# ConvNeXt block and Mamba block on one core: the first conv pairs written ahead of the weights' setup, and the first batch's MLP with its eight halves interleaved

## The chip, the core and the metric

The kernel runs on one core of one Trainium2 chip. A core has five engines with their own instruction queues: TensorE (PE, matrix products; its weight loads are listed as PEld), VectorE (DVE), ScalarE (ACT), GpSimd (POOL) and SyncE (SP), which here issues nearly all DMA transfers. Each engine works through its queue in order and waits on semaphores for the others. The metric is the device time in microseconds (us), smaller is better. The time before is 17438.78 us, the median of three runs (17432.75 to 17440.56).

## The reference

Two layers run one after the other on x of shape 32 x 96 x 56 x 56. The first is a ConvNeXt block, the second a Mamba block with two scan layers, a pooled branch, a 1x1 fusion and a batch norm. The change touches only the first layer:

```python
h = conv7x7_depthwise(x, conv_w) + conv_b          # one filter per channel
h = transpose(h, (0, 2, 3, 1))                     # channels last
h = (h - mean(h)) * rsqrt(var(h) + 1e-5) * ln_g + ln_b     # over the 96 channels
h = gelu(h @ w1 + b1)                              # 96 -> 384
h = h @ w2 + b2                                    # 384 -> 96
x = transpose(h, (0, 3, 1, 2)) * layer_scale + x
```

The second layer takes this x, batch by batch, through layer norm, projection, a causal conv of four taps, and a scan along the 3136 positions. Its pooled branch needs the mean of x over all positions of a batch.

## The kernel before

**Program order.** The kernel is written with a framework that orders the instructions of each engine at build time. Outside the loop that order is the framework's: of the instructions whose inputs are there it takes the one written first, so an instruction that waits for nothing can move far ahead of its place in the text. The loop at the end (L962 on) is under a manual order, in which the text is the order.

**Setup (L114 to L243).** Loads and prepares all weights: identity matrix, selection matrices, the layer norms' gains folded into the projections (`norm_weights`), the second layer's weights twice. Nearly all tiles are in the pool `const` and live to the end. Scratch is in `su`, with two PSUM banks in `sups`. Every transfer is issued by SP.

**First conv (L257 to L326).** The batches are split into groups: batches 0 to 10 (b0 = 11) first, then three groups of 7. For the first group the depthwise conv runs in front of the loop. The channels go in 48 pairs. For a pair p, 112 partitions hold two channels x 56 rows. A band matrix T of 112 x 7 x 112 holds the 7 x 7 filter (one 112 x 112 block per column offset dw). It is built on DVE with seven `copy_predicated` instructions, under seven masks that POOL makes once (three `affine_select` each, L269 to L277). Then PE multiplies, for two parts of the batches, seven shifted images with the seven blocks (L318), and ACT adds the bias and evicts (L322). The transfers of a pair are: the image into xpad (L302), the band out to DRAM for the later groups (L312) and the result out (L326). Band and image have three buffers each, used in turn. The conv's weights (cw, L288, and the bias cb, L289) are loaded with each filter repeated over the 56 rows. The pools `cc` (SBUF), `cx` and `cp` (six PSUM banks) open after the setup's pools are closed.

**MLP of a batch (`block0`, L383).** Batch b, chunk c (of four), half s (of two): 392 positions each. It is cut into pieces: load (conv result), load_x (input), center (L355), square (L360), mean (L365), root (Ln and Exp, L371 and L372), norm (L419), up (three products, L424), gelu (three activations, L432), down (L439 and L443), residual (L450, and the store of a chunk, L455). For the last half of a batch come total, pool and fuse, which make the pooled branch's bias `fb`. Each piece has a slot number, which says where in the loop it is put. For the batches 1 to 31 these pieces run inside the loop, one half per stage. For batch 0 they are written in front of the loop (L939), half by half, each half's pieces in the order of their slots. The tiles come from the loop's pool `wp` (cv, xin and gl with one buffer each) and from the loop's PSUM tags ps0, ps1 and ps2, with one bank each.

**First preparation and loop.** `prep` (L541) of the first stage runs next: it loads seq (the stored result of the MLP), norms and projects it. Then the loop runs 256 stages of 24 steps: each step is an Exp on ACT, a product and a scan on DVE (L878, L885) and a product on POOL (L889), and PE sums up (L922). The last part (L996 on) computes the batch norm and writes the output.

Of the kernel before, what the change touches and what calls it, by code (L numbers as in the profile page):

```python
# [34 lines left out]
F32 = mybir.dt.float32  # L35
I32 = mybir.dt.int32
AF = mybir.ActivationFunctionType
ALU = mybir.AluOpType
AX = mybir.AxisListType
PSUM = bass.MemoryType.PSUM  # L40
DRAM = bass.MemoryType.DRAM

H = W = 56
L = H * W
C = 96
# [6 lines left out]
NCH = 4  # L52
CH = L // NCH
HC = CH // 2
ROWS = HC // W
FF = 384
NF = FF // 128
# [4 lines left out]
def convnext_mamba_kernel(  # L62
# [31 lines left out]
    nc = tc.nc  # L94
# [3 lines left out]
    const = ctx.enter_context(tc.tile_pool(name="const", bufs=1))  # L98
# [3 lines left out]
    b0 = B - 3 * NB if B > 3 * NB else B  # L102
    groups = [(0, b0)] + [(b, b + NB) for b in range(b0, B, NB)]
    conv_d = [
        dram.tile([C * H, (hi - lo) * W], F32, name=f"conv_d{lo}", tag=f"conv_d{lo}")
        for lo, hi in groups
    ]
    band_d = dram.tile([C // 2, 2 * H, 7 * 2 * H], F32, name="band_d")
    stats_d = dram.tile([C, B * NCH, 4], F32, name="stats_d")
    x1_d = [dram.tile([C, L], F32, name=f"x1_d{b}", tag=f"x1_d{b}") for b in range(B)]  # L110
    o_d = [dram.tile([C, L], F32, name=f"o_d{b}", tag=f"o_d{b}") for b in range(B)]


    setup = ExitStack()  # L114
# [80 lines left out]
    for i in range(2):  # L195
# [12 lines left out]
        if i == 1:  # L208

            d["res"] = fw1  # L210
            for q in range(NQ):
                ps = sups.tile([128, 512], F32, name="ps", tag="nps")
# [40 lines left out]
        nc.vector.memset(t[C : C + 1, :], 1.0)  # L253
        hn0s.append(t)


    R2 = 2 * H  # L257
    GB = (b0 + 1) // 2
    cb = const.tile([R2, C // 2], F32, name="cb")
    with tc.tile_pool(name="cc", bufs=1) as cc, tc.tile_pool(name="cx", bufs=3) as cx, tc.tile_pool(  # L260
        name="cp", bufs=6, space=PSUM
    ) as cps:
        ones = cc.tile([R2, R2], F32, name="ones")
        nc.vector.memset(ones, 1.0)
        masks = []
        for dh in range(7):
            m = cc.tile([R2, R2], F32, name="m", tag="m", bufs=2)

            nc.gpsimd.affine_select(  # L269
                out=m, in_=ones, compare_op=ALU.is_equal, fill=0.0, base=3 - dh,  # L270
                pattern=[[-1, R2]], channel_multiplier=1,
            )
            nc.gpsimd.affine_select(
                out=m[:, 0:H], in_=m[:, 0:H], compare_op=ALU.is_ge, fill=0.0, base=H - 1,
                pattern=[[0, H]], channel_multiplier=-1,
            )
            nc.gpsimd.affine_select(  # L277
                out=m[:, H:R2], in_=m[:, H:R2], compare_op=ALU.is_ge, fill=0.0, base=-H,
                pattern=[[0, H]], channel_multiplier=1,
            )  # L280
            mi = cc.tile([R2, R2], I32, name=f"mi{dh}", tag=f"mi{dh}")
            nc.vector.tensor_copy(mi, m)
            masks.append(mi)
        cw = cc.tile([R2, C // 2, 49], F32, name="cw")
        wv = conv_w.rearrange("(p two) k -> two p k", two=2)
        bv = conv_b.rearrange("(p two) k -> two p k", two=2)
        for j in range(2):
            nc.sync.dma_start(cw[j * H : (j + 1) * H], wv[j].partition_broadcast(H))  # L288
            nc.sync.dma_start(  # L289
                cb[j * H : (j + 1) * H].unsqueeze(2), bv[j].partition_broadcast(H)  # L290
            )
        bands, xpads = [], []
        for i in range(3):
            t = cc.tile([R2, 7, R2], F32, name=f"band{i}", tag=f"band{i}")
            nc.gpsimd.memset(t, 0.0)
            bands.append(t)
            t = cc.tile([R2, b0, W + 6], F32, name=f"xpad{i}", tag=f"xpad{i}")
            nc.gpsimd.memset(t, 0.0)
            xpads.append(t)
        for p in range(C // 2):  # L300
            xp, T = xpads[p % 3], bands[p % 3]
            nc.sync.dma_start(  # L302
                xp[:, :, 3 : 3 + W],
                x[0:b0, 2 * p : 2 * p + 2, :].rearrange("b c (h w) -> (c h) b w", w=W),
            )
            for dh in range(7):
                nc.vector.copy_predicated(
                    T,
                    masks[dh].unsqueeze(1).broadcast_to([R2, 7, R2]),
                    cw[:, p, dh * 7 : (dh + 1) * 7].unsqueeze(2).broadcast_to([R2, 7, R2]),  # L310
                )
            nc.sync.dma_start(band_d[p], T.rearrange("p k n -> p (k n)"))  # L312
            ct = cx.tile([R2, b0 * W], F32, name="ct")
            for lo in range(0, b0, GB):
                n = min(GB, b0 - lo)
                ps = cps.tile([R2, GB * W], F32, name="ps")
                for dw in range(7):
                    nc.tensor.matmul(  # L318
                        ps[:, 0 : n * W], T[:, dw, :], xp[:, lo : lo + n, dw : dw + W],
                        start=(dw == 0), stop=(dw == 6),  # L320
                    )
                nc.scalar.activation(  # L322
                    ct[:, lo * W : (lo + n) * W], ps[:, 0 : n * W], AF.Identity,
                    bias=cb[:, p : p + 1],
                )
            nc.sync.dma_start(conv_d[0][p * R2 : (p + 1) * R2, :], ct)  # L326


    with ExitStack() as main:
        wp = main.enter_context(tc.tile_pool(name="wp", bufs=2))  # L330
        pp = main.enter_context(tc.tile_pool(name="pp", bufs=3, space=PSUM))
        pu = main.enter_context(tc.tile_pool(name="pu", bufs=1, space=PSUM))
        py = main.enter_context(tc.tile_pool(name="py", bufs=1, space=PSUM))
        bcd = main.enter_context(tc.tile_pool(name="bcd", bufs=3, space=DRAM))

        def psum(k):

            return pp.tile([128, 512], F32, name="ps", tag=f"ps{k}", bufs=1)

        def halves(t):  # L340
            return t.rearrange("p (a b) -> p a b", a=2)
# [14 lines left out]
            return ps  # L356

        def squared(ps):
            sq = wp.tile([R2, HC], F32, name="sq", tag="sq", bufs=3)[0:C]
            nc.scalar.activation(sq, ps[0:C, 0:HC], AF.Square)  # L360
            return sq

# [17 lines left out]
        batch_sums = {}  # L380
        xins = {}

        def block0(b, c, s):  # L383
# [2 lines left out]

            def load():
                if k == 0:
                    batch_sums[b] = wp.tile([C, NCH * 2], F32, name="sums", tag="sums", bufs=2)
                v["cv"] = wp.tile([C, ROWS, W], F32, name="cv", tag="cv", bufs=1)  # L390
                g = 0 if b < b0 else 1 + (b - b0) // NB
                at = (b - groups[g][0]) * W
                nc.sync.dma_start(
                    v["cv"],
                    conv_d[g].rearrange("(c h) w -> c h w", h=H)[
                        :, k * ROWS : (k + 1) * ROWS, at : at + W
                    ],
                )

            def load_x():  # L400
                if s == 0:
                    xins[b, c] = wp.tile([C, CH], F32, name="xin", tag="xin", bufs=1)
                    nc.sync.dma_start(xins[b, c], x[b, :, c * CH : (c + 1) * CH])

            def center():
# [21 lines left out]
                    )  # L427

            def gelu():
                v["gl"] = wp.tile([128, NF, HC], F32, name="gl", tag="gl", bufs=1)  # L430
                for f in range(NF):
                    nc.scalar.activation(  # L432
                        v["gl"][:, f], v["pss"][f][:, 0:HC], AF.Gelu, bias=b1_sb[:, f : f + 1]
                    )
                exp_ln_tables()
# [20 lines left out]


            def total():
                v["m"] = wp.tile([C, 1], F32, name="mean", tag="gps")
                nc.vector.tensor_reduce(v["m"], batch_sums[b], AX.X, ALU.add)  # L460

            def pool():
                ps = psum(2)
                nc.tensor.matmul(ps[0:C, 0:1], gpw_sb, v["m"], start=True, stop=True)
                v["gp"] = wp.tile([C, 1], F32, name="gp", tag="gps")
                nc.scalar.activation(v["gp"], ps[0:C, 0:1], AF.Relu, bias=gpb, scale=1.0 / L)

            def fuse():
                ps = psum(2)
                nc.tensor.matmul(ps[0:C, 0:1], fw2, v["gp"], start=True, stop=True)  # L470
                fb = wp.tile([C, 1], F32, name="fb", tag="fb", bufs=3)
                nc.scalar.activation(fb, ps[0:C, 0:1], AF.Identity, bias=fusb)
                batch_bias[b] = fb

# [3 lines left out]
                (12.8, root), (14.1, True, norm), (15.6, up), (15.9, gelu), (17.3, down),  # L478
                (18.3, residual),
            ]  # L480


        xpad = wp.tile([R2, NB, W + 6], F32, name="xpad", tag="xpad", bufs=1)
# [452 lines left out]
            for _, piece in sorted(where.pop(n, ()), key=lambda p: p[0]):  # L936
                piece()

        for c in range(NCH):  # L939
            for s in range(2):  # L940
                for slot, *piece in sorted(block0(0, c, s), key=lambda p: p[0]):
                    piece[-1]()
        for slot, *piece in sorted(prep(stages[0]), key=lambda p: p[0]):
            if slot < 24:
                piece[-1]()
# [143 lines left out]
```

## Time and profile before

| What | us |
|---|---|
| median of three runs | 17438.78 |
| the profiled execution | 17446.45 |
| its span | 17444.6 |
| up to the last setup transfer's issue | 48.73 |
| DVE's first band copy | 93.19 |
| PE's first conv product | 105.43 |
| first load of the MLP of batch 0 | 463.42 |
| last residual of batch 0 | 595.87 |
| first norm of the first preparation | 600.41 |
| first scan of the loop | 643.23 |

Times in the table are from the start of the profiled span. Over the whole span DVE is busy 92%, POOL 89%, PE 89% and ACT 66% of the time, but these are averages over stages with different limits. The stages in front of the loop have to be looked at by themselves. In the lines that follow, a name such as `ps<-cv,center_m` means output from inputs, with the buffers' numbers left out; `x8` counts instructions; the bracket at the end gives how long the engine was idle before, and what released it. Some names occur twice, as digits are left out: `cb<-in_conv_b` is the conv's bias, `cb<-in_mconv_b` that of the second layer. SPq is SP's queue: a transfer's time there is that of its issue, not of its data.

### The profile page before, as it was taken

To read this page: it belongs to the slowest core of one execution; us is meant where nothing else is said; L and a number is where in the kernel's file an instruction comes from. 1 tells how busy PE (TensorE), PEld (TensorE's weight loads), DVE (VectorE), ACT (ScalarE), POOL (GpSimd) and SP (SyncE) were. 2 spreads that over 40 slices of the span, in tenths; PEclk is the share of its full clock that TensorE was granted. 3 is DMA by queue.
4 is the path that set the end of the run, shared out by engine and by line. 5 is a ranking of instruction groups with operands and counts; after the bars stand their busy time and mean duration, and the time that the engine had idled before them with its cause. 6 is when DMAs were issued, how large, how long until landed. Compare 5 with 4: busy or idle time off the path is not lost. (4 is left out here: it accounts for less than half of the span.)

```text
span 17444.6 us, 217495 instructions
## 1 busy us (share of the span) xinstructions
PE 15502.9 (89%) x67992; PEld 5472.5 (31%) x67992; DVE 16064.8 (92%) x12345; ACT 11460.0 (66%) x18647; POOL 15605.6 (89%) x8737
## 2 busy tenths in 40 slices
PE   7799999999999999999999988888888888888870
PEld 5233333333333333333333322222222222222220
DVE  7499999999999999999999999999999999999994
ACT  1566766666666666666666666666666666666653
POOL 0499999999999999999999999999999999999991
PEclk9799999999999999999999999999999999999985
DMA  4355555555555555555555555555555555555548
GB/s 101 87 141 138 141 138 136 138 140 139 140 135 139 138 139 139 136 137 138 139 140 138 134 126 130 127 125 126 126 129 128 125 126 126 129 127 124 127 115 276
DMA packets 1421981, 2346.44 MB, mean 135 GB/s; under 512 B 629958, under 2 KB 793586, under 8 KB 1420820
## 3 DMA queue, kind: packets, MB, share of 16 engines
q1 hardware_dynamic: 1413652, 2294.00, 53.7%
q10 hardware_dynamic: 7168, 38.54, 0.6%
q8 instruction: 536, 8.78, 0.2%
q14 instruction: 625, 5.12, 0.1%
HBM read 1929.11 MB, written 402.41 MB: 134 GB/s over the span
## 5 line engine op out<-in xcount | busy, mean ns | idle before, releaser
L889 POOL TENSOR_TENSOR da<-h,bc 128x784 f32<-128x784 f32 x6144 | 11267.2, 1856 | 855.6 <-DVE h L885 734.9
L885 DVE TENSOR_TENSOR_SCAN h<-da,st,w 128x784 f32<-128x784 f32 x3072 | 5664.5, 1844 | 326.4 <-ACT st L896 8.6
L922 PE MATMUL y<-da,ssum 128*32 128x392 f32 x24576 | 5147.1, 542 | 407.2 <-POOL da L889 403.2
L878 DVE TENSOR_TENSOR w<-w,bc 128x784 f32<-128x784 f32 x4096 | 3996.2, 976 | 300.9 <-PE w L851 132.7
L862 POOL TENSOR_TENSOR da<-us,bc 128x784 f32<-128x784 f32 x2048 | 3819.1, 1865 | 2.3 <-DMA us<-uu 2.3
L836 ACT ACTIVATE da<-d,A 128x784 f32<-128x784 f32 x4096 | 3757.4, 941 | 43.1 <-DMA d<-dd 27.3
L836 ACT ACTIVATE w<-d,A 128x784 f32<-128x784 f32 x2048 | 1878.3, 918 | 2635.0 <-DVE h L885 2285.8
L885 DVE TENSOR_TENSOR_SCAN h<-w,st,da 128x784 f32<-128x784 f32 x1536 | 2712.2, 1827 | 5.9 <-ACT w L836 4.8
L587 PE MATMUL ps<-hn,wx 97*64 97x392 f32 x12288 | 2265.9, 503 | 7.4 <-DVE hn L575 7.4
L922 PEld LDWEIGHTS y<-da,ssum 128*32 128x32 f32 x24576 | 1094.8, 115 | 3681.1 <-issue 2141.1
L885 DVE TENSOR_TENSOR_SCAN h<-da,w 128x784 f32<-128x784 f32 x1024 | 1827.0, 1784 | 109.1 <-ACT st L896 4.3
L851 PE MATMUL w<-u,sel 64*128 64x392 f32 x4096 | 1026.5, 580 | 655.0 <-DVE h L885 654.0
L587 PEld LDWEIGHTS ps<-hn,wx 97*64 97x64 f32 x12288 | 793.7, 137 | 1434.5 <-issue 1117.3
L666 POOL TENSOR_TENSOR u<-dl,xc 128x784 f32<-128x784 f32 (+1 forms) x512 | 737.5, 1440 | 564.1 <-ACT dl L652 564.1
L916 PE MATMUL y<-xc,D 128*128 128x392 f32 x1536 | 802.2, 608 | 257.1 <-DVE z L903 249.4
L506 PE MATMUL ps<-xpad,band 112*112 112x224 f32 (+1 forms) x4032 | 1003.0, 358 | 0.0
L351 ACT ACT_TABLE_LOAD x759 | 973.8, 1283 | 14.3 <-PEq L1076 0.8
L885 DVE TENSOR_TENSOR_SCAN h<-w,da 128x784 f32<-128x784 f32 x512 | 872.3, 1766 | 0.0
L360 ACT ACTIVATE sq<-ps 96x392 f32<-96x392 f32 x768 | 340.7, 490 | 797.3 <-PE ps L355 448.9
L506 PEld LDWEIGHTS ps<-xpad,band 112*112 112x112 f32 x4032 | 583.7, 175 | 832.5 <-issue 770.0
L644 PE MATMUL ps<-dbl,dtw 6*64 6x392 f32 x3072 | 685.7, 509 | 99.6 <-ACT dbl L622 99.6
L851 PEld LDWEIGHTS w<-u,sel 64*128 64x128 f32 x4096 | 327.9, 196 | 1255.6 <-DVE h L885 1096.3
(124 smaller groups left out, 14444.6 us busy)
## 6 DMA issues: line engine op xcount, KB each, us to landing
bc<-bd SPq DMA_DIRECT2D x4096, 196.0 KB, 5.3
d<-dd SPq DMA_DIRECT2D x6144, 98.0 KB, 2.9
us<-uu SPq DMA_DIRECT2D x2048, 98.0 KB, 2.2
dd<-dl SPq DMA_DIRECT2D x512, 294.0 KB, 3.8
uu<-u SPq DMA_DIRECT2D x1024, 49.0 KB, 1.6
band<-band_d SPq DMA_DIRECT2D x144, 343.0 KB, 3.6
cv<-conv_d SPq DMA_DIRECT2D x256, 147.0 KB, 2.5
xin<-in_x SPq DMA_DIRECT2D x128, 294.0 KB, 4.2
```

Of the source, the lines that this page charges most:

```text
L351: nc.scalar.preload_act_table_set("natural_log_exp_and_others")
L506: nc.tensor.matmul(v["ps"][0:R2, 0 : (last - first) * W], v["band"][:, dw, :], xpad[:, first:last, dw : dw + W], start=(dw == 0), stop=(dw ...
L587: nc.tensor.matmul(v["x", q][rows(a), 0:HC], weights[:, k, 64 * q : 64 * q + 64], v["hn"][:, o : o + HC], start=(k == 0), stop=(k == last),)
L666: nc.gpsimd.tensor_tensor(S.u[:, lo:hi], v["dl"][:, lo:hi], S.xc[:, lo:hi], ALU.mult)
L836: nc.scalar.activation(e, S.d4[j], AF.Exp, scale=S.d["A"][:, j, g : g + 1])
L851: nc.tensor.matmul(S.u4[:, 512 * a : 512 * a + HC], sel[rows(a), j % 2, :], S.u[rows(a), j // 2, :], start=True, stop=True,)
L862: nc.gpsimd.tensor_tensor(t, S.us[j], S.bcs[g][:, 0, :], ALU.mult)
L878: nc.vector.tensor_tensor(halves(db), S.u4.rearrange("p (a b) -> p a b", a=2)[:, :, 0:HC], halves(S.bcs[g][:, 0, :]), ALU.mult,)
L885: nc.vector.tensor_tensor_scan(ring[:, g, :], S.e.pop((j, g)), db, 0.0 if c == 0 else d["st"][:, j, g : g + 1], ALU.mult, ALU.add,)
L889: nc.gpsimd.tensor_tensor(da, ring[:, g, :], S.bcs[g][:, 1, :], ALU.mult)
L916: nc.tensor.matmul(S.y[:, 0:HC], S.d["D"][:, q, :], S.xc[:, q, :], start=True, stop=False)
L922: nc.tensor.matmul(S.y[r0 : r0 + 32, 0:HC], ssum, da[:, tok(a)], start=False, stop=(g == NG - 1),)
```

## The change

The block of the first conv, from its pools up to the images' memsets, moves ahead of the setup, and the body of its loop over pairs becomes a function `conv_pair(p)`. Three pairs are written before the setup, the other 45 after it. The pools stay open in between, beside those of the setup, in an `ExitStack`. The MLP of batch 0 gets an SBUF pool `p0` with three buffers for each of its tiles and a PSUM pool `pp0` with eight banks of one tag, which are closed before the loop's pools are opened. Its pieces are no longer written half after half. All are sorted by their slot plus 3 for each half.

```diff
+    first_conv = ExitStack()
+    cc = first_conv.enter_context(tc.tile_pool(name="cc", bufs=1))
+    cx = first_conv.enter_context(tc.tile_pool(name="cx", bufs=3))
+    cps = first_conv.enter_context(tc.tile_pool(name="cp", bufs=6, space=PSUM))
...
+    for j in range(2):
+        nc.sync.dma_start(cw[j * H : (j + 1) * H], wv[j].partition_broadcast(H))
+        nc.sync.dma_start(
+            cb[j * H : (j + 1) * H].unsqueeze(2), bv[j].partition_broadcast(H)
+        )
...
+    def conv_pair(p):
+        xp, T = xpads[p % 3], bands[p % 3]
...
+    for p in range(3):
+        conv_pair(p)
+
+
     setup = ExitStack()
     su = setup.enter_context(tc.tile_pool(name="su", bufs=2))
     sups = setup.enter_context(tc.tile_pool(name="sups", bufs=2, space=PSUM))
...
-        for p in range(C // 2):
-            xp, T = xpads[p % 3], bands[p % 3]
...
+    for p in range(3, C // 2):
+        conv_pair(p)
+    first_conv.close()
...
     with ExitStack() as main:
-        wp = main.enter_context(tc.tile_pool(name="wp", bufs=2))
-        pp = main.enter_context(tc.tile_pool(name="pp", bufs=3, space=PSUM))
-        pu = main.enter_context(tc.tile_pool(name="pu", bufs=1, space=PSUM))
-        py = main.enter_context(tc.tile_pool(name="py", bufs=1, space=PSUM))
-        bcd = main.enter_context(tc.tile_pool(name="bcd", bufs=3, space=DRAM))
-
+        pre = []
         def psum(k):
 
+            if pre:
+                return pre[1].tile([128, 512], F32, name="ps", tag="pre", bufs=8)
             return pp.tile([128, 512], F32, name="ps", tag=f"ps{k}", bufs=1)
+
+        def work(shape, name, bufs):
+
+            pool, n = (pre[0], 3) if pre else (wp, bufs)
+            return pool.tile(shape, F32, name=name, tag=name, bufs=n)
...
-                v["cv"] = wp.tile([C, ROWS, W], F32, name="cv", tag="cv", bufs=1)
+                v["cv"] = work([C, ROWS, W], "cv", 1)
...
-                v["gl"] = wp.tile([128, NF, HC], F32, name="gl", tag="gl", bufs=1)
+                v["gl"] = work([128, NF, HC], "gl", 1)
...
-                fb = wp.tile([C, 1], F32, name="fb", tag="fb", bufs=3)
+                fb = (
+                    const.tile([C, 1], F32, name="fb0")
+                    if pre
+                    else wp.tile([C, 1], F32, name="fb", tag="fb", bufs=3)
+                )
...
+        with tc.tile_pool(name="p0", bufs=1) as p0, tc.tile_pool(
+            name="pp0", bufs=1, space=PSUM
+        ) as pp0:
+            pre += [p0, pp0]
+            pieces = [
+                (slot + 3 * (2 * c + s), piece)
+                for c in range(NCH)
+                for s in range(2)
+                for slot, *_, piece in block0(0, c, s)
+            ]
+            for _, piece in sorted(pieces, key=lambda p: p[0]):
+                piece()
+            pre.clear()
+
+        wp = main.enter_context(tc.tile_pool(name="wp", bufs=2))
+        pp = main.enter_context(tc.tile_pool(name="pp", bufs=3, space=PSUM))
...
-        for c in range(NCH):
-            for s in range(2):
-                for slot, *piece in sorted(block0(0, c, s), key=lambda p: p[0]):
-                    piece[-1]()
         for slot, *piece in sorted(prep(stages[0]), key=lambda p: p[0]):
```

The lines left out move unchanged. xin, sums, sq, and the two small tiles of the pooled branch are switched to `work` in the same way as cv and gl.

## The prediction

> **What bounds the kernel now.** I read three views, from coarse to fine. First, the busy time of each engine in stretches that I cut at the kernel's own joints: setup, the convolution's weights, the first conv pairs, the conv, the MLP of batch 0, the first preparation, the loop. Columns: microseconds from the span's start, length, then busy time (and instruction count) of each engine, granted TensorE clock, DMA share, GB/s.
>
> ```profile
> core 0: us, PE busy (x) PEld busy (x) DVE busy (x) ACT busy (x) POOL busy (x), PEclk, DMA share, GB/s
> 0.00:48.73 48.73, 7.22 (x20) 2.97 (x20) 11.69 (x46) 2.36 (x6) 0.70 (x6) 1.00 0.20 38
> 48.73:93.19 44.46, 0.59 (x4) 0.30 (x4) 3.88 (x14) 0.85 (x4) 8.15 (x27) 1.00 0.30 34
> 93.19:105.43 12.24, 0.00 (x0) 0.03 (x1) 12.24 (x14) 0.00 (x0) 0.00 (x0) 1.00 0.28 36
> 105.43:463.42 357.99, 354.74 (x1344) 236.55 (x1344) 330.25 (x323) 49.71 (x96) 0.00 (x0) 1.00 0.45 119
> 463.42:596.36 132.94, 90.50 (x151) 35.69 (x152) 4.88 (x9) 60.69 (x88) 0.00 (x0) 0.63 0.12 30
> 596.36:640.00 43.64, 34.30 (x130) 13.05 (x129) 2.39 (x5) 24.21 (x36) 1.84 (x1) 0.73 0.39 100
> 640.00:17240.00 16600.00, 15015.56 (x66348) 5183.90 (x66345) 15632.83 (x11899) 11259.58 (x18383) 15594.92 (x8703) 0.94 0.55 134
> ```
>
> The loop is 16600 of 17444.6 us, held by DVE and POOL (both 94%), and the change does not write into it. What it touches is the first 640 us: 93 us in which no compute engine does much, 358 us of conv with PE full, and 133 us of MLP in which nothing is full (PE 68% at a granted clock of 0.63, ACT 46%). All of it precedes the loop's first scan (643.23), so what is saved there is saved at the end.
>
> Second, the timeline at the start of the conv (start, duration, engine, line, operation; in brackets the idle time before and its releaser):
>
> ```profile
> 48.73 13.00 SPq L289 DMA_DIRECT2D cb<-in_conv_b  x2
> ...
> 62.05 24.15 SPq L288 DMA_DIRECT2D cw<-in_conv_w  x2
> 86.24 6.71 SPq L302 DMA_DIRECT2D xpad<-in_x  x3
> 93.19 7.39 DVE L307 COPY_PREDICATED band<-mi,cw 112x784 f32<-112x784 int32 x8 [33.99 <-DMA cw<-in_conv_w]
> ...
> 116.10 0.33 SPq L302 DMA_DIRECT2D xpad<-in_x  x1
> ```
>
> SP's queue is the limit here: setup's transfers are issued from 0.80 to 48.7 without a break (48 us), then 44 us for bias, conv weights and the first three images. DVE waits 34 us for cw.
>
> Third, one half of the MLP:
>
> ```profile
> 483.58 1.28 ACT L371 ACT_TABLE_LOAD   x1
> ...
> 484.87 0.55 ACT L371 ACTIVATE ps<-ps,eps_c 96x392 f32<-96x392 f32 x1
> 485.44 1.28 ACT L372 ACT_TABLE_LOAD   x1
> 486.74 0.47 ACT L372 ACTIVATE ps<-ps 96x392 f32<-96x392 f32 x1
> 487.23 1.28 ACT L432 ACT_TABLE_LOAD   x1
> 487.25 0.56 DVE L419 TENSOR_TENSOR hz<-cv,ps 96x392 f32<-96x392 f32 x1 [15.59 <-ACT ps L372]
> 487.86 0.50 PEld L424 LDWEIGHTS ps<-hz,w_sb 97*128 97x128 f32 x2 [4.00 <-DVE hz L419]
> 487.86 4.29 PE L424 MATMUL ps<-hz,w_sb 97*128 97x392 f32 x6 [3.35 <-DVE hz L419]
> ...
> 498.01 0.58 ACT L450 ACTIVATE xin<-ps,b2ls 96x392 f32<-96x392 f32 x1 [5.24 <-PE ps L443]
> ```
>
> It is one chain: each engine waits for the one before, and the next half's center waits for this residual, since both use the PSUM tile of tag ps2. A half lasts 18.5 us the first time and 16.4 on average after (463.42 to 596.36: 132.9 = 18.5 + 7 x 16.4).
>
> **The conv's weights first.** Issue of cw, cb, cw, cb costs 24.15 + 13.00 = 37.2 us wherever it stands; moved to the head it runs from 0.8 to 38. The second cw is through after 0.8 + 12.1 + 6.5 + 12.1 = 31.5 and lands 7 us later, as now (86.2 to 93.19): copies from about 38.5 instead of 93.2, the three image loads from 38 to 44.7, PE 12.2 us after the copies (as now, 93.19 to 105.43) at 50.7. The three pairs take 22 us (a pair is 7.33: ACT's rows of L322 repeat every 7.32), to 73. POOL's 27 mask and memset instructions (8.15 us) move under the wait for cw; the ident that setup needs stands behind them, but setup's transfers are issued only 40 us later, so this is free.
>
> But setup's 48 us of issue did not go away. It is written ahead of pairs 3 to 47, and its transfers wait for nothing, so I take them to stand on SP before the image of pair 3: 44.7 + 48 + six stores of pairs 0 to 2 (0.3 to 0.4 each, 2 us) = 95, plus 4.3 us to land (the median of that load) = 99. Pair 3 starts now at 105.43 + 22 = 127.4. Gain 28. DVE executes in order, and setup's last operations wait for the last setup transfers; if copies for pair 3 stand behind them they start at 97 and pair 3 at 104 or later. Setup's other DVE work (46 instructions, 11.7 us, till now under DMA waits) fits into the idle time from 73 to 97; without that cover it costs its 11.7 us, since in the conv DVE is 92% busy. PE's and ACT's setup work (7 and 2 us) lies in the same gap. **I take 25**. Ends: 0, if setup's transfers or its DVE work stand ahead of pair 0 (SP then ends where it ends now); 42, if the images of pairs 3 and on slip between setup's transfers (105.4 - 50.7 less 12 for DVE).
>
> The pools cost nothing: conv and setup now hold 6 + 2 PSUM banks together, and conv's memsets no longer wait for setup's tiles.
>
> **The MLP interleaved.** Tiles get 3 buffers and 8 PSUM tiles, and pieces are sorted 3 slots apart, so two to three halves are under way at once. The chain no longer decides, the fullest engine does. ACT per half: 0.49 (square) + 0.55 + 0.47 + 3 x 0.59 (gelu) + 0.58 + 0.19 (residual) = 4.05, and three table loads of 1.28 = 3.85: 7.9, which the window of each half confirms. PE: 18 passes of 0.33 us at full clock (the second center to down of 576.98 on) = 5.9, of 0.65 at half clock = 11.8.
>
> Two rules bear on this. The row first: a table load takes 1.28 us and the Ln after it starts 10 ns later. The Trainium skill, "ScalarE: Activation LUTs", section on what ACT_TABLE_LOAD costs, gives 1283 ns plus a drain of about 1380, and advises to do all work of one set before switching; interleaving does the opposite. With 2.66 us per switch a half would be 4.05 + 8.0 = 12 and the saving at the stage's end 31; with the row's 1.28 it is 59. The row decides, as no such drain shows in it. The advice keeps its point, though: gelus of one half come 0.65 us apart on PE, and the next half's Ln or Exp can fall between them; each such break is one more 1.28. At most five loads per half (Ln, Exp and three gelus all apart) give 10.5. I count one extra: **9.2 us per half**.
>
> The clock: now PE idles 3.35 us before each up, and up's passes run at 0.65. "TensorE: Matmul & The Clock Gate", Part 1, says the clock halves after an idle window of some 3.4 us and comes back after a busy one; with no such gap left PE would need 5.9 per half and ACT alone would bind. The row nearest in density, 596 to 640 (PE 79% busy), was granted only 0.73, where 18 passes last 0.33 / 0.73 x 18 = 8.1. Both are under 9.2, so I keep 9.2; only at half clock throughout would PE set 11.8.
>
> Sum: first half 18.5, then 7 x 9.2 = 64.4, together 83 instead of 133: 50 saved. Ends: 7.9 per half, 59; 11.8, 32.
>
> **What is given back.** Now the first preparation (seq loads, center, square, mean) runs inside the last half: center<-seq at 589.8, and its first norm at 600.41, 4 us after the residual. In the change the loop's pools open after the MLP's close, so seq's load waits for fuse: total, pool and fuse 2 us, load 2.5, center to Exp 5.5 (1.3 + 0.5 + 1.3 + 0.55 + 1.28 + 0.47): norm at 10 us after the residual. **Minus 6** (2 to 10). The fb0 tile and the hoisted preloads (L351, one load at 0.80) cost nothing.
>
> **Sum:** 25 + 50 - 6 = 69. The profiled execution took 17446.45 us (span 17444.6, 1.85 around it), 7.7 over the median of the runs, 17438.78; its 69 come off the median: **17370**.
>
> **Rivals.** *Forecast* as above, 0.60, its own range 17350 to 17390. *Conv runs through*: SP leaves room for the later images; 42 + 50 - 6 = 86, 17353. For it: SP needs only 1.15 us per pair; against: order of writing. 0.16. *PE stays slow and setup goes first*: PE at half clock, 32, minus 6, plus 5: 31, 17408. For it: a clock of 0.60 in four of the eight halves; against: the 3.35 us gaps go. 0.14. *The halves stay in sequence* (some shared tile, such as hz, still ties them; hz has two buffers by s, and half k + 2 waits for up of half k): only setup's 25 less 10, 17424. 0.06. *Slower*: the loop. DVE and POOL are both 94% busy there, so anything that lengthens their instructions goes straight to the end. The loop's tiles may sit at other addresses after p0's; L862 and L889, the same POOL multiply on other tiles, differ by 9 ns already (1865, 1856). 11 ns on each of L889's 6144 eats the 69; at 20 ns it is 123, 17493. Against: order and sizes of the tiles are the same. 0.04.
>
> A difference under 0.2% (35 us) is what a measurement of this kernel cannot tell from none. Faster: 0.60 + 0.16 + two thirds of 0.14 = 0.86; same: the rest of that and 0.06, 0.10; slower 0.04. The range 17338 to 17412 leaves out the last two rivals and the ends of the others.
>
> **What would show it.** cw at the head of SP's queue and copies near 38; a PE gap between pairs 2 and 3, ending near 99; conv's last store near 435; eight residuals 9 us apart; more than three table loads in some halves; granted clock above 0.7 in that stage; a first norm 10 us after the last residual; a loop as long as now. Wrong it is if x of pair 3 is issued before setup's transfers, if the halves' distance is 8 or 12, or if the loop's length moves by tens of microseconds.

## The result, and the profile after

| | before | after |
|---|---|---|
| median of four runs each | 17439.67 (17432.75 to 17445.83) | 17358.18 (17343.56 to 17373.99) |
| ratio | 1 | 0.9954 (0.9936 to 0.9971) |
| the profiled execution (its span) | 17446.45 (17444.6) | 17343.56 (17341.9) |
| DVE's first band copy | 93.19 | 25.29 |
| PE's first conv product | 105.43 | 43.89 |
| first load of the MLP of batch 0 | 463.42 | 436.31 |
| last residual of batch 0 | 595.87 | 519.27 |
| first norm of the first preparation | 600.41 | 534.04 |
| first scan of the loop | 643.23 | 574.21 |

The changed kernel is 81.5 us faster in the medians. At the first scan it is 69.0 us ahead. The profiled execution of after is the fastest of its four, so its span alone shows more (102.7 us: 69.0 up to the first scan, 25.8 in the loop, 7.9 behind the last scan); the difference behind the first scan is looked at below.

The busy times of after, cut at the new joints: conv weights, first copies, pairs 0 to 2, the gap before pair 3, the rest of the conv, the MLP, the first preparation. Columns as before: start and end, length, busy time and count of each engine, granted TensorE clock, DMA share, GB/s.

```profile
core 0: us, PE busy (x) PEld busy (x) DVE busy (x) ACT busy (x) POOL busy (x), PEclk, DMA share, GB/s
0.00:25.29 25.29, 0.00 (x0) 0.00 (x0) 6.18 (x25) 1.28 (x1) 8.88 (x33) 1.00 0.33 42
25.29:43.89 18.60, 0.00 (x0) 0.03 (x1) 13.74 (x15) 0.00 (x0) 0.00 (x0) 1.00 0.28 37
43.89:68.00 24.11, 24.11 (x85) 15.87 (x86) 15.28 (x22) 2.07 (x4) 0.00 (x0) 1.00 0.42 102
68.00:100.90 32.90, 6.18 (x25) 2.86 (x24) 18.13 (x39) 2.85 (x10) 0.00 (x0) 0.56 0.28 64
100.90:436.31 335.41, 332.13 (x1260) 221.57 (x1260) 302.08 (x296) 46.61 (x90) 0.00 (x0) 0.99 0.45 120
436.31:519.94 83.63, 63.91 (x144) 29.27 (x144) 4.47 (x8) 62.17 (x89) 0.00 (x0) 0.80 0.16 40
519.94:574.21 54.27, 40.28 (x148) 18.33 (x150) 3.71 (x7) 23.51 (x36) 1.83 (x1) 0.72 0.44 107
```

Three rows matter. In 68 to 100.9 PE works 6 of 33 us, between pair 2 and pair 3. The MLP's row is 83.6 us long where it was 132.9, at a granted clock of 0.80 where it was 0.63, while ACT's busy time is as before (62.2 against 60.7): the same work, less waiting. The last row, from the last residual's end to the first scan, is longer than before (54.3 us against 46.9, 596.36 to 643.23): this is what was given back.

The timeline of after at the start (start, duration, engine, line, operation, and in brackets the idle time before and its releaser):

```profile
0.80 0.44 SPq L146 DMA_DIRECT2D cw<-in_conv_w  x1
...
1.29 2.20 SPq L147 DMA_DIRECT2D cb<-in_conv_b  x1
...
3.54 10.03 SPq L146 DMA_DIRECT2D cw<-in_conv_w  x1
...
13.61 9.86 SPq L147 DMA_DIRECT2D cb<-in_conv_b  x1
...
23.52 18.58 SPq L160 DMA_DIRECT2D xpad<-in_x  x3
25.29 13.74 DVE L165 COPY_PREDICATED band<-mi,cw 112x784 f32<-112x784 int32 x15 [14.09 <-DMA cw<-in_conv_w]
...
43.89 24.14 PE L176 MATMUL ps<-xpad,band 112*112 112x336 f32 x84 [43.89 <-DMA xpad<-in_x]
...
97.53 0.32 SPq L160 DMA_DIRECT2D xpad<-in_x  x1
...
100.90 29.34 PE L176 MATMUL ps<-xpad,band 112*112 112x336 f32 x101 [2.43 <-DMA xpad<-in_x]
```

The four weight transfers are through SP at 23.5, not 38, and the three images take SP 18.6 us, not 6.7. The image of pair 3 is issued at 97.5, behind all of the setup, and PE goes on 3.4 us later.

One half of the MLP in after, ACT only:

```profile
465.81 1.28 ACT L381 ACT_TABLE_LOAD   x1
467.11 0.56 ACT L381 ACTIVATE ps<-ps,eps_c 96x392 f32<-96x392 f32 x1
467.68 1.28 ACT L442 ACT_TABLE_LOAD   x1
468.97 0.59 ACT L442 ACTIVATE gl<-ps,b_sb 128x392 f32<-128x392 f32 x1
469.58 1.28 ACT L382 ACT_TABLE_LOAD   x1
470.87 0.47 ACT L382 ACTIVATE ps<-ps 96x392 f32<-96x392 f32 x1
471.37 1.28 ACT L442 ACT_TABLE_LOAD   x1
472.66 1.06 ACT L442 ACTIVATE gl<-ps,b_sb 128x392 f32<-128x392 f32 x2
473.62 0.49 ACT L370 ACTIVATE sq<-ps 96x392 f32<-96x392 f32 x1
475.09 0.58 ACT L460 ACTIVATE xin<-ps,b2ls 96x392 f32<-96x392 f32 x1 [0.98 <-PE ps L453]
```

A gelu of the half in front falls between Ln and Exp of the half behind: four table loads, one more than before. ACT has almost no idle time left; only the residual still waits for PE, here 0.98 us.

The end of the MLP in after:

```profile
519.27 0.58 ACT L460 ACTIVATE xin<-ps,b2ls 96x392 f32<-96x392 f32 x1 [2.05 <-PE ps L453]
...
521.23 0.26 ACT L486 ACTIVATE fb<-ps,fusb 96x1 f32<-96x1 f32 x1 [0.42 <-PE ps L480]
...
522.64 0.77 SPq L585 DMA_DIRECT2D seq<-x_d  x2
522.93 0.42 DVE L519 MEMSET xpad<- 112x434 f32 x1 [2.81 <-DMA x_d<-xin]
...
526.12 2.90 PE L365 MATMUL ps<-seq,center_m 96*96 96x392 f32 x4 [4.93 <-DMA seq<-x_d]
...
534.04 1.03 DVE L610 TENSOR_TENSOR hn<-seq,ps 96x392 f32<-96x392 f32 x2 [10.69 <-ACT ps L382]
```

`seq` is not issued when fuse is done (521.5) but at 522.6, and the center that reads it starts at 526.1. What SP waited for was the landing of the MLP's last store (`x_d<-xin`, issued at 520.0): the trace puts 2.1 us of SP's wait down to it, and DVE's next instruction, a memset into the loop's pools, is released by it too. So the closed pool is free only when its last reader, that store, is through.

### The profile page after: what moved, and what is told of

Its sections match the earlier page's. It is cut to its first block, busy times and chain, and to the rows that moved or that the text cites. A ratio compares the mean times of both kernels' runs of the same rounds, so it can differ in the third digit from the quotient of the medians.

```text
span 17341.9 us, 217468 instructions
## 1 busy us (share of the span) xinstructions
PE 15452.2 (89%) x67992; PEld 5467.0 (32%) x67992; DVE 16061.7 (93%) x12345; ACT 11459.0 (66%) x18648; POOL 15637.1 (90%) x8737
## 5 line engine op out<-in xcount | busy, mean ns | idle before, releaser
L924 POOL TENSOR_TENSOR da<-h,bc 128x784 f32<-128x784 f32 x6144 | 11295.2, 1861 | 799.0 <-DVE h L920 686.1
```

The lines of the kernel that those rows point to most:

```text
L924: nc.gpsimd.tensor_tensor(da, ring[:, g, :], S.bcs[g][:, 1, :], ALU.mult)
```

## The experiments

Theory A is the sum of the prediction: two savings at the head and in the MLP that pass undiminished through the loop. Its rivals differ from experiment to experiment. The table has all runs, with the number of executions behind each median in brackets; first scan and loop are of the profiled execution (us from the start of the span; loop from its first to its last scan).

| run | median us (executions) | ratio | first scan | loop |
|---|---|---|---|---|
| conv_only | 17401.12 (20) | 0.9978 (0.9971 to 0.9984) | 618.77 | 16428.6 |
| mlp_only | 17383.86 (9) | 0.9972 (0.9962 to 0.9982) | 598.57 | 16432.1 |
| after_again | 17354.81 (4) | 0.9953 (0.9937 to 0.9970) | 573.54 | 16414.7 |
| before_again | 17445.19 (1) | | 644.74 | 16429.1 |
| mlp_in_sequence | 17397.84 (1) | | 600.90 | 16431.1 |
| all_pairs_first | 17338.80 (4) | 0.9942 (0.9926 to 0.9959) | 554.06 | 16416.6 |
| act_in_order | 17337.15 (4) | 0.9939 (0.9924 to 0.9954) | 549.97 | 16427.2 |
| seq_apart | 17358.01 (1) | | 569.74 | 16417.7 |
| combined | 17302.37 (5) | 0.9923 (0.9910 to 0.9935) | 523.71 | 16400.0 |
| cb_first | 17434.97 (12) | 1.0000 (0.9991 to 1.0009) | 642.37 | 16402.4 |
| head_later | 17443.94 (20) | 1.0006 (1.0000 to 1.0013) | 648.95 | 16422.4 |

The medians of before beside them were 17439.13 for the first four runs, 17443.27 for the next four and 17437.53 for the last three.

### Each part alone

Only the conv is moved; the MLP stays as before, in the loop's pools and half after half (edit against after):

```diff
-            pieces = [
-                (slot + 3 * (2 * c + s), piece)
-                for c in range(NCH)
-                for s in range(2)
-                for slot, *_, piece in block0(0, c, s)
-            ]
-            for _, piece in sorted(pieces, key=lambda p: p[0]):
-                piece()
...
+        for c in range(NCH):
+            for s in range(2):
+                for slot, *piece in sorted(block0(0, c, s), key=lambda p: p[0]):
+                    piece[-1]()
```

> Only the conv's half of the change: its weights and three pairs ahead of the setup; the MLP of batch 0 as before, in the loop's pools and half by half. Theory (the parts add up, each at its own stage): the first load of the MLP comes at 436, 27 us earlier than before, the MLP still takes 132 us and its first norm still comes 4.5 us after the last residual, so the first scan comes at 616 and the time falls by 27. Rival (part of the conv's gain only shows because the MLP was rewritten too, for instance because its input loads now have more buffers): first load later than 440 and a gain under 15.

Only the MLP is changed; the conv stays behind the setup (edit against after):

```diff
-    for p in range(3):
-        conv_pair(p)
-
-
     setup = ExitStack()
...
+        for p in range(C // 2):
+            xp, T = xpads[p % 3], bands[p % 3]
```

> Only the MLP's half: own pools and interleaved halves; setup and conv as before. Theory: first load at 463 as before, 83 us from there to the last residual, first norm 14.8 us after it, the stretch from first norm to first scan 40 instead of 43: first scan at 601, 42 us earlier than before. Rival (the interleave owes some of its speed to the conv's move, for instance through the TensorE clock at its start): the MLP takes over 90 us here.

The MLP's first load came at 436.8 with the conv alone (436 expected), and its stage took 81.0 us with the MLP alone (83 expected, over 90 by the rival), so neither rival holds. At the first scan the conv alone is 643.23 - 618.77 = 24.5 us ahead, the MLP alone 44.7. Together that is 69.2, and both at once gave 69.0. In the medians it is 38 and 55 us, together 93, against 84 for the whole change beside the same executions of before (after_again). So at the first scan the parts add: neither gives back what the other gains. The medians show more than the first scan does, which leads to the next question.

### The loop: cause or chance?

In the two profiled executions the loop was 16430.2 us before and 16404.4 after, though the change writes nothing into it. Both kernels were profiled once more, unchanged.

> The changed kernel once more. Theory A (the part of the gain that the prediction didn't have, 12 us in the median and 34 in the profiled execution, is chance in the loop): the stretch before the first scan is again 574 within 1 us, and the loop from first to last scan differs from the profiled 16404 by ten us or more in one or the other direction, with the time at half clock in the loop going the same way. Theory B (the change shortens the loop by itself, for instance through other tile addresses): the loop is again 16404 within 5 us.

> The kernel before once more, for its loop. Theory A (chance): first scan at 643 within 1 us, the loop from first to last scan anywhere from 16395 to 16445, where the profiled execution had 16430. Theory B (the loop before is longer by itself): 16430 within 5 us.

The loop of after now took 16414.7, with 27 us more at half clock: by the expectation that speaks for chance. That of before took 16429.1, which fits both theories, so this run alone decides nothing. Of the 25.8 us of difference 14.4 are left, in the same two kernels. Over the 13 profiled executions of this study loop lengths lie between 16400 and 16432, with and without the change at both ends (combined has 16400 and cb_first, which is before with one tile declared earlier, 16402; mlp_only has 16432 and before 16430). The windows of the loop, after and then before, show where it sits:

```profile
574.21:16978.60 16404.39, 14978.63 (x66305) 5177.12 (x66302) 15577.48 (x11855) 11207.79 (x18343) 15622.07 (x8701) 0.94 0.54 133
```

```profile
643.23:17073.40 16430.17, 15005.51 (x66302) 5180.85 (x66300) 15577.81 (x11855) 11208.48 (x18343) 15590.63 (x8701) 0.94 0.54 132
```

DVE's and ACT's busy times agree within 0.7 us, so they did the same work at the same pace. POOL's is 31 us higher in the shorter loop, most of it in one line, L889 before and L924 after (one row of each profile page, before and then after):

```profile
L889 POOL TENSOR_TENSOR da<-h,bc 128x784 f32<-128x784 f32 x6144 | 11267.2, 1856 | 855.6 <-DVE h L885 734.9
```

```profile
L924 POOL TENSOR_TENSOR da<-h,bc 128x784 f32<-128x784 f32 x6144 | 11295.2, 1861 | 799.0 <-DVE h L920 686.1
```

This goes with the change: POOL's busy time in the loop is 15611 to 15626 us in the eight executions with the MLP in pools of its own and 15588 to 15591 in the five without. What lengthens it is open (the profiler's spans on POOL are rough), but it does not show in the loop's length, 16418 us on average in the eight and 16423 in the five. In after POOL waits less instead (799 us before this line, not 856). PE's busy time is 27 us higher in the longer loop, about the difference, and PE's is the one that goes with the granted clock (a pass of the MLP's up takes 0.65 us at half clock, 0.33 at full). Added up from the clock records, PE stood at half clock for 1894 us in this loop of after and for 1980 in that of before. Over the 13 executions this time runs from 1853 to 1980 us and goes with the loop's length, with a correlation of 0.90 and 0.26 us of loop per us at half clock. That is a correlation; no run set the clock by itself.

Two more runs asked whether an address or the start time of the loop could do it. First, before with `cb` at the place in its pool that it has in after:

```diff
+    cb = const.tile([2 * H, C // 2], F32, name="cb")
...
-    cb = const.tile([R2, C // 2], F32, name="cb")
```

> The kernel before with one tile, the conv's bias, declared first in its pool: every address in that pool moves, nothing else. The changed kernel, each of its halves and two variants all spent 16782 to 16787 us (median time less the profiled first scan) behind the first scan, the kernel before 16795. Theory A (that difference of 11 us comes with the addresses): 17428 or less. Theory B (chance or the head's timing): 17436 to 17443.

Second, before with a later head, by a setup transfer that is issued eight times more:

```diff
+    for _ in range(8):
+        nc.sync.dma_start(g0, ln0_g)
```

> The kernel before with one small load in the setup (the first norm's gain) repeated eight times, which holds SP for about 16 us near the start and moves all behind it. Theory A (when the loop starts changes how long it lasts): the time less the first scan is 16790 or less. Theory B (it doesn't): it stays 16795 within 4 us, and the time goes up by as much as the first scan moves, about 16 us.

The first changed nothing (17434.97, ratio 1.0000), though its profiled execution, the fastest of the twelve, had a loop of 16402: a short loop comes without the change. The second put the first scan only 4 to 6 us later than in the two profiles of before, not 16, since most of the added transfers slipped between others; the median rose by 6 us. That agrees with a later head costing just its delay, but the interval of the ratio (up to 1.0013, 23 us) is wide, and the test smaller than planned. Neither run shows a dependence of the loop. What stays open: the median less the first scan is 16793 to 16796 us for before, cb_first and head_later, and 16779 to 16787 for the kernels that hold a part of the change (medians of four or more executions). These 10 us, 0.06% of the time, have no cause here; executions of one kernel differ by 20 to 43.

### The MLP: the pools or the order?

The pools of after, with the halves one after the other:

```diff
-                (slot + 3 * (2 * c + s), piece)
+                (slot + 100 * (2 * c + s), piece)
```

> The changed kernel, but with the MLP's pieces of batch 0 written half after half as before; its own pools stay, with three buffers each and eight PSUM banks. Theory (the order in which the pieces are written makes the interleave): only the next half's center and square slip ahead of a half's residual, three table loads per half, a half takes 14 to 15 us and the stage from first load to last residual 116 to 122. Rival (the buffers make it, since outside the loop the framework orders by what is ready): 83, give or take 5.

The first load came at 435.6 and the last residual at 546.8, so the stage took 111.2 us: 21.3 less than before, 28.2 more than after, and a little less than the 116 to 122 expected. Of the 49.5 us the pools alone bring 21.3, the order the other 28.2; the rival, that the buffers alone make it, does not hold. Between two residuals (timeline of this run, rows chosen):

```profile
465.68 0.58 ACT L460 ACTIVATE xin<-ps,b2ls 96x392 f32<-96x392 f32 x1 [1.49 <-PE ps L453]
466.38 1.28 ACT L381 ACT_TABLE_LOAD   x1
...
470.05 0.56 DVE L429 TENSOR_TENSOR hz<-cv,ps 96x392 f32<-96x392 f32 x1 [12.95 <-ACT ps L382]
...
476.05 1.20 PE L365 MATMUL ps<-cv,center_m 96*96 96x392 f32 x2
477.29 0.49 ACT L370 ACTIVATE sq<-ps 96x392 f32<-96x392 f32 x1 [1.71 <-PE ps L365]
479.26 0.58 ACT L460 ACTIVATE xin<-ps,b2ls 96x392 f32<-96x392 f32 x1 [1.48 <-PE ps L453]
```

A half takes 479.26 - 465.68 = 13.6 us where it took 16.4. The center and the square of the next half (476.05, 477.29) now run ahead of this half's residual (479.26), because they no longer share a PSUM tile with it. The rest of the half is still one chain: Ln, Exp, norm, up, gelu, down.

### The table loads

The same pieces in the same order, but ACT's own order is held as written, and the framework no longer lets a ready gelu pass:

```diff
-            for _, piece in sorted(pieces, key=lambda p: p[0]):
-                piece()
+            with tc.manual_schedule(engines={mybir.EngineType.Activation}):
+                for _, piece in sorted(pieces, key=lambda p: p[0]):
+                    piece()
```

> The changed kernel with ACT's order in the MLP of batch 0 held to the written one: square, residual, Ln and Exp side by side, then the three gelus, and the preload of the table for Ln and Exp after them, so two table loads per half instead of four. Theory (ACT with its table loads sets the distance of the halves): ACT per half falls from 9.2 to 6.6, the stage from 83 to 65 (62 to 70), and the first preparation saves up to 2.6 more as it finds the table loaded. Rival (PE at a clock of 0.7 to 0.75 sets it): the stage takes 75 or more, a gain under 10.

One half of it, ACT only:

```profile
463.99 1.28 ACT L361 ACT_TABLE_LOAD   x1
465.28 0.49 ACT L370 ACTIVATE sq<-ps 96x392 f32<-96x392 f32 x1
465.68 0.57 ACT L460 ACTIVATE xin<-ps,b2ls 96x392 f32<-96x392 f32 x1
...
466.76 0.55 ACT L381 ACTIVATE ps<-ps,eps_c 96x392 f32<-96x392 f32 x1 [0.42 <-PE ps L375]
467.35 0.47 ACT L382 ACTIVATE ps<-ps 96x392 f32<-96x392 f32 x1
467.84 1.28 ACT L442 ACT_TABLE_LOAD   x1
469.14 1.54 ACT L442 ACTIVATE gl<-ps,b_sb 128x392 f32<-128x392 f32 x3
470.70 1.28 ACT L361 ACT_TABLE_LOAD   x1
```

The three gelus stand together, and Ln and Exp need one load for both: the one that the kernel asks for at L361, which now stays in its place instead of moving to the head of the program. Two loads per half instead of four, 465.7 to 472.4 between residuals (6.7 us) instead of 10.3. The stage fell from 83.0 to 61.8 us (65 expected, 62 to 70), and the first scan came 24 us earlier; the rival, PE at its lower clock, would have left 75 or more. Of the 3.6 us per half 2.6 are the two loads. The other 1.0 is shorter waiting, and the run doesn't separate what ACT's order and what PE's higher clock (1.00 where it was 0.83) do to that. ACT's loads, and the waits that go with them, were what set the distance in after. Now PE is as full as ACT: from 452.7 to 497.0 ACT is busy 41.5 and PE 40.9 of 44.3 us.

### The gap between pair 2 and pair 3

All 48 pairs are written ahead of the setup:

```diff
-    for p in range(3):
+    for p in range(C // 2):
         conv_pair(p)
...
-    for p in range(3, C // 2):
-        conv_pair(p)
```

> The changed kernel with all 48 conv pairs written ahead of the setup instead of three. Theory (PE's idle time from 68 to 101 is there because setup's transfers are written ahead of the image of pair 3 and hold SP): the images now go out between setup's transfers, the gap closes but for the 12 us of setup's DVE work, which the conv no longer hides; the MLP's first load comes at 412 (405 to 418) instead of 436, and the first scan 20 to 28 us earlier. Rival (SP's issue itself is the limit, so the same sum of transfers takes as long in any order): first load at 430 or later.

Its window from 68 to 100.9, cut like that of after:

```profile
68.00:100.90 32.90, 25.34 (x92) 16.18 (x91) 24.98 (x29) 4.45 (x11) 0.00 (x0) 0.94 0.51 128
```

And two lines of SP in its timeline:

```profile
72.84 0.48 SPq L160 DMA_DIRECT2D xpad<-in_x  x1
73.37 0.98 SPq L302 DMA_DIRECT2D dtw<-in_dt_w  x1
```

PE now works 25 us between 68 and 100.9 instead of 6; images (xpad) are issued between the setup's loads (dtw). The conv's last product ended at 409.0 instead of 433.0 and the MLP's first load came at 412.4 (412 expected, 430 or later by the rival). The first scan came 20 us earlier, as the MLP's stage took 87.0 us instead of 83.0 here. So the gap in after is the setup's transfers standing in front of one image by the order of writing. The setup's 48 us of issue can run beside the conv.

### The first preparation's load

The first stage's center and norm read a second copy of the same chunk, loaded into a tile that no pool boundary holds back:

```diff
+                    if S is stages[0]:
+                        v["src"] = hns[1][0:C, 3 : 3 + CH]
+                        nc.sync.dma_start(v["src"], x1_d[b][:, c * CH : (c + 1) * CH])
...
-                v["ps"] = [centred(S.seq[:, tok(a)], a) for a in range(2)]
+                v["ps"] = [centred(v.get("src", S.seq)[:, tok(a)], a) for a in range(2)]
```

> The changed kernel, but the first preparation reads its chunk from a second copy in memory that is free all the while (rows of the second layer's norm output, used first two stages later), loaded as soon as the MLP has stored it; seq itself is loaded as before. Theory (the first norm comes 14.8 us after the last residual instead of 4.5 because seq's load waits until the MLP's pools are free): center no longer waits for that load, and the first norm comes 10 us after the last residual (9 to 11). Rival (the PSUM banks or the order on PE hold it): still 14 to 15.

```profile
520.96 0.58 ACT L460 ACTIVATE xin<-ps,b2ls 96x392 f32<-96x392 f32 x1 [2.05 <-PE ps L453]
...
522.92 0.26 ACT L486 ACTIVATE fb<-ps,fusb 96x1 f32<-96x1 f32 x1 [0.42 <-PE ps L480]
...
523.23 2.10 PE L365 MATMUL ps<-hn,center_m 96*96 96x392 f32 x4 [0.35 <-ACT fb L486]
...
530.21 1.03 DVE L614 TENSOR_TENSOR hn<-hn,ps 96x392 f32<-96x392 f32 x2 [5.17 <-ACT ps L382]
```

This is the timeline of seq_apart. The first norm comes 9.2 us after the last residual (10 expected, 14 to 15 by the rival). The center now starts 2.3 us after the last residual's start instead of 6.9, released by `fb`, the last user of the MLP's PSUM pool. First scan 569.74, 4.5 us earlier in the profile. The load behind the pool's end was on the path; what is left is the PSUM pool, which can't open before fuse. The one time of this run (17358.01) is within the spread of after's.

### All three together

> The changed kernel with all 48 conv pairs ahead of the setup, ACT in the written order in the MLP of batch 0, and the first preparation's chunk read from the second copy. Theory (the three gains lie one behind the other on the path to the first scan): 20 + 24 + 4.5 = 48 us before the changed kernel's first scan, 526, and a time of 17310. Rival (they overlap: ACT's order already gave 2.3 of the time to the first norm, and what comes later is late next): first scan at 535 or later, 17320 or more.

The three edits gave 20.2, 24.2 and 4.5 us at the first scan by themselves, 48.9; together the first scan came at 523.71 (526 expected, 535 by the rival), 50.5 us before that of after. So they lie one behind the other on the path. The median is 17302.37, ratio 0.9923 (0.9910 to 0.9935) to before. This version beats both kernels, by about 135 and 55 us.

## Why the prediction was right, step by step

**The conv part** was 27.1 us at the MLP's first load; 28 was the sum and 25 was taken, for DVE work whose cost does not show in the end. The mechanism held: the order of writing on SP put the setup in front of pair 3, and all_pairs_first shows that it was the cause. That the working on SP came out near is in part luck, as two errors in it cancelled. The duration of a transfer's issue was carried over from its old place: cw and cb were to hold SP for 37.2 us wherever they stand. They held it for 22.7, with no setup transfers under way in front of them. The images behind them took 18.6 instead of 6.7, so PE started at 43.9, not at 50.7. Both together ended at 42.1 on SP, against the predicted 44.7. This didn't move the end, since pair 3 hung on the setup's last transfer: 97.5 (95 forecast), PE at 100.9 (99). "Its transfers wait for nothing" was not quite so: one, `raw` of the second layer, waited for 2.8 us (87.6 to 90.4), and what stood behind it on SP with it.

**The MLP part** was 49.5 us in the stage against 50, and its mechanism was as told: no half waits for another, a gelu falls between Ln and Exp, and every half has four loads once the halves run side by side. That the size came out so near is in part luck again: the 9.2 per half was too small in the middle, and the end was forgotten. Between residuals 454.0 and 516.0 it is 62.0 / 6 = 10.3 us: ACT busy 9.0, and 1.4 us idle, nearly all of it where the residual waits for its down. The last residual follows after 3.3 us, as nothing stands behind it. First half 17.7, six of 10.3, one of 3.3: 83.

**Table loads.** Each is 1.28 us and the next activation starts 10 to 20 ns after its end, as the row of before said. With the 2.66 us that the Trainium skill ("ScalarE: Activation LUTs", what ACT_TABLE_LOAD costs) gives with its drain, the four of a half would be 10.6 and the half 14.7; it took 10.3. The page's advice on doing the work of one set together ("Rules for kernel authors") was right all the same: act_in_order is that, and it brought 24 us.

**The clock** in the stage rose from 0.63 to 0.80. PE was fuller than before but not the bound: from 454.0 to 516.0 it was busy 47.1 us and ACT 53.8 of 62.0.

**Given back:** the first norm came 14.8 us after the last residual where it was 4.5, so 10.2 us later where 6 was taken. The load's start was too small: the working had it wait for fuse only, but its pool also waits for the last store, 1.1 us more. The load took 3.5 from issue to use instead of 2.5. The largest miss is center to norm, 7.9 instead of 5.5: the working followed one half of the chunk, but ACT does the squares of both halves before its load for Ln (529.6), and both Ln before its load for Exp (532.3). Most of that is made good at once. In before the second norm came 3.8 us behind the first:

```profile
600.41 0.56 DVE L575 TENSOR_TENSOR hn<-seq,ps 96x392 f32<-96x392 f32 x1 [3.68 <-ACT ps L372]
...
604.23 0.56 DVE L575 TENSOR_TENSOR hn<-seq,ps 96x392 f32<-96x392 f32 x1 [3.26 <-ACT ps L372]
```

In after it comes 0.5 us behind (the x2 at 534.04 above), with one table load between the two norms instead of three. From the second norm to the first scan all kernels here take 39.0 to 40.5 us, but for combined with 37.9. So at the first scan 7.6 us were given back, not 10.2: the 6 came near because one error made up for a good part of another.

**The sum** at the first scan is 27.1 + 49.5 - 7.6 = 69.0, as forecast, but 81.5 in the medians. The range held it. By number alone 17358 lies nearer to the 17353 of the rival *conv runs through* than to 17370; the trace decides against that rival, as pair 3's image went out at 97.5, behind the setup. It was right about what SP can do, as all_pairs_first shows, and wrong about what the order of writing lets it do. The prediction's own sign of being wrong, a loop that moves by tens of microseconds, did appear in the first two profiles (25.8 us); by the runs above it is mostly chance, and about 10 us stays open. *The slower loop* did not come, but its first step did: POOL's L889 takes 5 ns longer in the profile of after. The step that failed is "goes straight to the end": 31 us more of POOL's time do not show in the loop's length, though POOL is 94% busy there.

## What to carry to other kernels

Work that is moved to the head of a queue pushes back what it passes: look for the first thing that still hangs behind the old work (here one image behind 48 us of setup transfers), because that, and not the new start, sets the gain. When a chain of short steps is opened by interleaving, the next bound is the fullest engine with its switches counted; hold that engine's order by hand if the framework may mix kinds of work on it. A pool that closes in front of the next stage is freed by its last store, so what the next stage needs first should not live behind that boundary.

## What was unexpected in the hardware

A transfer's time in SP's queue is not its own cost. In after the first load of cw held SP for 0.44 us and the second, of the same size, for 10.03. The same four loads of cw and cb took 37.2 us of issue behind the setup and 22.7 in front of it, and three image loads 6.7 us or 18.6. The queue seems to be held by the transfers ahead of it, which no run tested by itself; here the sum over the issue times held better than its terms (43.9 before, 41.3 after).

In the clock records of these traces the stretches at half clock are multiples of 3.41 us, and their phase against the start of the program differs between executions. In the loop, stages of 63.6 and of 66.1 us occur in one and the same execution, with about 5 and 11 us at half clock. This goes with the spread of some 15 us up and down in a loop of 16.4 ms, and it bounds what a single profile can say of a change this small.
